# Batch 0's rows of three experts moved into the routing of batch 1, in a Perceiver layer with a mixture of experts

## Chip, cores and metric

The kernel runs on one core of a Trainium2 chip, in one launch. The metric is the device time of that core in microseconds (us). Before the change the median of three runs is 2997.42 us (2994.43 to 2998.41).

## What is computed

One layer in three steps, each added to x (2 batches of 512 tokens, 512 channels, float32): cross-attention to 8192 context tokens, causal self-attention, and a mixture of 16 experts with two experts for each token. The change lies in the third step:

```python
cap = int(LOAD * K * max(1, T / E))                      # 64 places for each expert and batch
g = jnp.einsum('btc,ce->bte', x, w_router)               # x: after a layer norm
gate_probs = jax.nn.softmax(g, axis=-1)
top_k_probs, positions, indices, expert_inputs = jax.vmap(lambda xb, pb: _dispatch(xb, pb, cap))(x, gate_probs)
expert_inputs = jnp.swapaxes(expert_inputs, 0, 1).reshape(E, B * cap, C)
gg = jnp.einsum('enc,ech->enh', expert_inputs, w_gate)
h = jnp.einsum('enc,ech->enh', expert_inputs, w_fc)
h = jax.nn.silu(gg) * h
o = jnp.einsum('enh,ehc->enc', h, w_proj)
expert_outputs = jnp.swapaxes(o.reshape(E, B, cap, C), 0, 1)
y = jax.vmap(_collect)(expert_outputs, indices, positions, top_k_probs)   # weighted sum of two rows per token
```

A token gets a place in its expert by counting along the batch, so the places of a batch are known only when all its tokens have been routed. Each expert has 64 places for batch 0 and 64 for batch 1, 128 rows together.

## The kernel before

**The stages.** Cross-attention fills the first 2500 us or so, self-attention the next 300 (`self_attention`, L1148). Batch 0's routing (`route(0, ...)`, L756) is cut into pieces that are hung into the gaps of batch 1's self-attention (`attend(1, fill)`, L1536). Then the routing of batch 1 runs by itself (`in_line`, L895), the rows of all experts are fetched (L1540), the experts run one after another (`experts`, L936), and at the end each token gathers its two result rows.

**What sets the order.** Each engine works through its own queue in program order, which is the order in which the Python code records the instructions. Engines wait for each other through semaphores that the tile framework puts in where one reads what another writes, or where a buffer is used again. DMAs are issued from three queues: SP (weights, stores of normed rows, final output), ScalarE (result rows of the experts), POOL (the indirect ones, which pick rows by number).

**Routing of batch 1** (`in_line`). For each of four tiles of 128 tokens: the last projection of self-attention (`output`), the statistics of the layer norm, and one call of `between(i)`, which loads an expert's weights. The first three tiles are normed on ScalarE, stored to the tensor `normed` in HBM (L770) and turned on TensorE (`turn`, L193, four 128x128 transposes into a bank, which is then copied to SBUF); the last tile follows. The router (L792) multiplies the turned tokens, 128 at a time as the stationary operand, with the 16 columns of the router's weights. Then come the two best experts of each token on VectorE (`top_first`, `top_second`), the counting of places on TensorE (`counted`, L840 to L845), on VectorE a one-hot of the places (`ranked`, L849), and on TensorE the token number of each place (`numbered`, L876), which is written to `mo.token`: 64 rows for batch 0, 64 for batch 1, one column for each expert. `probabilities` ends it, and a tiny sigmoid (L923) loads ScalarE's table for the experts.

**Fetch** (L927). For each expert one indirect DMA on POOL picks the 128 rows named in its column of `mo.token` from `normed` into a quarter of a buffer `gx` (four buffers with four experts each).

**Experts** (L936). For each expert the rows are turned (`turned_tile`), multiplied with the gate weights `wg` and the weights `wf` (`expand`, L953: the weights are the stationary operand, 128x128 each, the 128 rows the moving columns), a sigmoid on ScalarE and two products on VectorE make `hT`, and `contract` (L966) multiplies it with `wp`, copies the result to SBUF and writes 64 rows to `results[0]` and 64 to `results[1]` in HBM. The loop turns two experts ahead and contracts one behind. A matmul in float32 shows in the trace as two passes, each with its own weight load: 32 passes for an expansion, four for a contraction.

**Weights and buffers.** `load(e)` (L715) takes three buffers of the pool `mid` (22 buffers of 128x1024 float32), freed in the order in which their last readers stand. Experts 0 to 2 are loaded early (L1514), 3 to 5 by `between` in the routing, and six ahead in the loop (L986). The pool `big` has ten buffers (`gx`, `xn`, `mxnT` and the exponentials of the attention). In the self-attention and the routing PSUM is a ring of eight banks (`Ring`, L200); the experts have their own PSUM pool, which takes the banks over.

**End.** After the last expert's results have landed, POOL gathers for batch 0, then for batch 1, for each of four tiles twice 128 rows (L998); VectorE adds each, weighted, to `xs` (L1001), and SP writes out each tile (L1002).

The calls that put the stages in order are these (from L1536):

```python
attend(1, fill)
assert not pieces
in_line = route(1, bank, "j", bank, split=True)
in_line(lambda i: output(1, i), lambda i: load(3 + i) if i < 3 else None)
for e in range(E):
    fetch(e)
```

Of the kernel before, what the change touches and what calls it, by code (L numbers as in the profile page):

```python
# [11 lines left out]
F32 = mybir.dt.float32  # L12
# [3 lines left out]
AF = mybir.ActivationFunctionType  # L16
# [26 lines left out]
def perceiver_kernel(ctx: ExitStack, tc: tile.TileContext, a, out: bass.AP):  # L43
# [668 lines left out]
    NQ = 4  # L712
    loaded, pk, get, gx = {}, {}, {}, []

# [41 lines left out]
    def route(b, ps, pstag, ps1, split=False):  # L756
# [91 lines left out]

        def ranked():  # L849

# [9 lines left out]
            for k in range(2):  # L860
                nc.vector.tensor_tensor(
                    hit[:, k],
                    pos[:, k].unsqueeze(2).to_broadcast([P, TB, CAP]),
                    mo.place.unsqueeze(1).to_broadcast([P, TB, CAP]),
                    ALU.is_equal,
                )
            nc.vector.tensor_reduce(slot, both, AX.X, ALU.add)

# [25 lines left out]

        def in_line(output, between):  # L895

            last = TB - 1
            for i in range(TB):
# [12 lines left out]
            tiles.normed(last)  # L911
            stored(last)

            def halves(dst, src):
                nc.scalar.copy(dst[:, :2], src[:, :2])
                nc.vector.tensor_copy(dst[:, 2:], src[:, 2:])

            turn(ps, pstag, tiles[last], mxnT[:, :, last * P :], halves)
            router()
            for f in found:  # L920
                f()

            nc.scalar.activation(tile("warm", [P, 1]), eps, AF.Sigmoid)  # L923

        return in_line if split else pieces + [router, *found]

    def fetch(e):  # L927

        q, i = divmod(e, NQ)
        if i == 0:  # L930
            gx.append(b8("gx", (P, NQ, D)))
        nc.gpsimd.indirect_dma_start(
            out=gx[q][:, i, :], out_offset=None, in_=normed, in_offset=at_row(mo.token[:, e : e + 1])
        )

    def experts():  # L936
        with ExitStack() as st:
# [3 lines left out]
            def turned_tile(e):  # L941
                q, i = divmod(e, NQ)
                bT = sm.tile([P, ND, P], F32, tag="bT", name="bT", bufs=3)
                turn(ps, "t", gx[q][:, i, :], bT, nc.vector.tensor_copy)
                return bT

            def expand(e, bT):
                wg, wf, _ = loaded[e]
                ph = ps.tile([P, 2, NF, P], F32, tag="a", name="ph")
                for j, w in enumerate((wg, wf)):  # L950
                    for f in range(NF):
                        for c in range(ND):
                            nc.tensor.matmul(  # L953
                                ph[:, j, f, :],
                                w[:, c, f * P : (f + 1) * P],
                                bT[:, c, :],
                                start=(c == 0),
                                stop=(c == ND - 1),
                            )
                hT = sm.tile([P, NF, P], F32, tag="hT", name="hT")  # L960
                nc.scalar.activation(hT, ph[:, 0], AF.Sigmoid)
# [4 lines left out]
            def contract(e, hT):  # L966
                wpj = loaded.pop(e)[2]
                po = ps.tile([P, D], F32, tag="o", name="po2")
                for f in range(NF):
                    nc.tensor.matmul(po, hT[:, f, :], wpj[:, f, :], start=(f == 0), stop=(f == NF - 1))  # L970
                res = sm.tile([P, D], F32, tag="res", name="res")
                nc.scalar.copy(res, po)
                for b in range(B):
                    nc.scalar.dma_start(
                        results[b][e * CAP : (e + 1) * CAP, :], res[b * CAP : (b + 1) * CAP, :]
                    )

            turned = {0: turned_tile(0), 1: turned_tile(1)}
            before_h = None
            for e in range(E):  # L980
# [3 lines left out]
                if before_h is not None:  # L984
                    contract(e - 1, before_h)
                    if e - 1 + NBUF < E:  # L986
                        load(e - 1 + NBUF)
                before_h = hT
            contract(E - 1, before_h)


            for b in range(B):
                for i in range(TB):
                    y = xs[:, b * TB + i, :]
                    pair = m4("r", (P, 2, D))
                    for k in range(2):
                        r = pair[:, k, :]
                        nc.gpsimd.indirect_dma_start(  # L998
                            out=r, out_offset=None, in_=results[b], in_offset=at_row(get[b][:, k, i : i + 1])
                        )  # L1000
                        nc.vector.scalar_tensor_tensor(y, r, pk[b][:, k, i : i + 1], y, ALU.mult, ALU.add)  # L1001
# [146 lines left out]
    def self_attention(finish_cross, mo_w):  # L1148
        with ExitStack() as st:
# [363 lines left out]
            first_maxima(1, *(lambda i=i: output(0, i) for i in range(4)))  # L1513
            for e in range(3):  # L1514
                load(e)
# [22 lines left out]
            in_line = route(1, bank, "j", bank, split=True)  # L1538
            in_line(lambda i: output(1, i), lambda i: load(3 + i) if i < 3 else None)
            for e in range(E):  # L1540
                fetch(e)

    finish_cross = cross_attention(xattn_tail)
# [38 lines left out]
```

## Time and profile before

| What | us |
|---|---|
| median of three runs (lowest, highest) | 2997.42 (2994.43, 2998.41) |
| the profiled execution's own time | 2998.28 |
| its span (first to last instruction) | 2996.6 |
| TensorE busy in it | 2912.9 |
| VectorE, ScalarE, POOL busy | 1960.1, 1397.1, 2177.5 |
| mean granted TensorE clock | 0.987 |
| first fetch of rows starts (L932) | 2855.29 |
| first row turned for an expert (L193) | 2859.16 |
| last result write issued (L974) | 2965.3 |
| first and last final gather start (L998) | 2967.91, 2988.38 |

A row of the time line names the start, the length, the engine, the line of the kernel, the operation, what is written and read, and how often; in brackets stands how long the engine was idle before it and what ended that. PE is TensorE's matmul, PEld its weight load, DVE VectorE, ACT ScalarE, SP the DMA queue on SyncE. A queue's name ends in q. In a row by stretch each engine's busy time is followed by its number of instructions; then come the granted TensorE clock (1.00 is full, 0.50 half), the DMA engines' busy share and what they moved in GB/s. The ends of matmuls are modelled, so the spacing of starts says more than a row's length.

### The profile page before, as it was taken

What the parts mean: (1) busy time and instruction counts of PE and PEld (TensorE: products, weight loads), DVE (VectorE), ACT (ScalarE), POOL (GpSimd) and SP (SyncE); (2) the same over time, 40 slices, a digit from 0 to 9 for tenths busy, and PEclk for the clock granted to TensorE, in tenths of its full rate; (3) what the DMA queues carried; (4) which work ended last, traced back from release to release, by engine and by line L of the source; (5) the groups of instructions that cost most, each with busy time, mean ns of one, the idle gap of its engine ahead of it and who ended that gap; (6) DMA issues with size and microseconds to landing.
All of it is one profiled execution on the core that took longest, in us unless ns stands there. A gap on an engine that the chain in (4) does not pass through costs nothing.

```text
span 2996.6 us, 65645 instructions
## 1 busy us (share of the span) xinstructions
PE 2912.9 (97%) x28459; PEld 1128.1 (38%) x28459; DVE 1960.1 (65%) x3292; ACT 1397.1 (47%) x2614; POOL 2177.5 (73%) x880
## 2 busy tenths in 40 slices
PE   7999999999999999999999999999999999999985
PEld 2333333333333333333333333333333332345574
DVE  5567776677777677766777777777767666556422
ACT  1345555555555555544555555555555436563311
POOL 1598888888888888978888888888888872012022
PEclk9999999999999999999999999999999999999988
DMA  3000000000000000000000000000000002001374
GB/s 124 1 24 2 24 2 24 1 24 2 24 3 23 5 21 9 17 1 24 2 24 1 24 1 24 1 24 1 24 2 1 29 29 72 1 29 62 103 249 138
DMA packets 48145, 89.73 MB, mean 30 GB/s; under 512 B 4720, under 2 KB 23152, under 8 KB 47856
## 3 DMA queue, kind: packets, MB, share of 16 engines
q1 hardware_dynamic: 40832, 70.31, 7.0%
q0 software_dynamic: 2752, 8.39, 0.9%
q10 hardware_dynamic: 4272, 6.83, 0.7%
q8 instruction: 223, 3.65, 0.5%
q14 instruction: 66, 0.54, 0.1%
HBM read 77.13 MB, written 8.39 MB: 29 GB/s over the span
## 4 chain that ended last, share of the span: by engine, by line
PE 93%; DVE 3%; ACT 1%; DMA 1%; issue 1%; POOL 0%; ACTq 0%; POOLq 0%; DVEq 0%
PE s L220 31%; PE s L449 18%; PE s L514 16%; PE s L462 15%; PE s L481 4%; PE s L1244 2%; PE ph L953 2%; PE s L541 2%; PE po L970 1%; DVE cm L471 1%; PE s L1338 1%; PE s L1379 1%; DVE acc L549 1%; DMA r<-results,get 0%; DVE acc L529 0%
## 5 line engine op out<-in xcount | busy, mean ns | idle before, releaser
L680 POOL TENSOR_TENSOR es<-es,e 128x2048 f32<-128x2048 f32 x374 | 1700.7, 4547 | 54.9 <-ACT e L483 38.1
L483 ACT ACTIVATE e<-s 128x512 f32<-128x512 f32 x2048 | 1057.4, 603 | 1111.0 <-PE s L481 1111.0
L471 DVE TENSOR_REDUCE cm<-s 128x1 f32<-128x512 f32 x2048 | 1271.0, 683 | 332.3 <-PE s L449 332.2
L449 PE MATMUL s<-k,qT 32*128 32x512 f32 x4096 | 588.1, 641 | 3.4 <-DVE cm L471 1.9
L462 PE MATMUL s<-qT,k 32*128 32x512 f32 x4096 | 554.8, 593 | 3.1 <-ACT e L483 2.3
L514 PE MATMUL s<-e,v 128*32 128x512 f32 x4096 | 495.3, 600 | 1.1 <-DVE cm L471 1.0
L680 POOL TENSOR_TENSOR es<-e 128x2048 f32<-128x2048 f32 x63 | 286.1, 4541 | 242.9 <-ACT e L483 242.9
L220 PE MATMUL s<-wkv,ctx 128*32 128x512 f32 x3072 | 365.4, 596 | 0.4
L220 PE MATMUL s<-ctx,wkv 128*32 128x512 f32 x3072 | 356.5, 597 | 0.5
L462 PEld LDWEIGHTS s<-qT,k 32*128 32x128 f32 x4096 | 282.3, 184 | 185.1 <-issue 106.3
L529 DVE TENSOR_TENSOR acc<-acc,s 128x512 f32<-128x512 f32 (+1 forms) x359 | 207.8, 604 | 138.6 <-PE s L514 138.1
L449 PEld LDWEIGHTS s<-k,qT 32*128 32x128 f32 x4096 | 161.8, 183 | 330.7 <-issue 259.0
L514 PEld LDWEIGHTS s<-e,v 128*32 128x32 f32 x4096 | 107.4, 109 | 320.0 <-DVE cm L471 160.9
L481 PE MATMUL s<-rows,mb 4*128 4x512 bf16 x2048 | 218.0, 376 | 0.0
L425 DVE SCALAR_TENSOR_TENSOR k<-s,kf,m 128x512 f32<-128x512 f32 x128 | 96.1, 751 | 171.7 <-PE s L220 171.7
L220 PEld LDWEIGHTS s<-ctx,wkv 128*32 128x32 f32 x3072 | 87.2, 109 | 236.5 <-issue 155.5
L220 PEld LDWEIGHTS s<-wkv,ctx 128*32 128x32 f32 x3072 | 86.9, 109 | 214.3 <-issue 125.9
L440 ACT COPY v<-s 128x512 f32<-128x512 f32 x128 | 74.9, 585 | 98.7 <-PE s L220 77.8
L537 DVE TENSOR_TENSOR acc<-acc,s 128x1024 f32<-128x1024 f32 x56 | 68.4, 1221 | 71.1 <-ACT s L536 71.1
L1325 POOL TENSOR_SCALAR_AFFINE_SELECT e<-e 128x512 f32<-128x512 f32 x32 | 22.3, 708 | 120.0 <-ACT e L1323 120.0
L481 PEld LDWEIGHTS <-mb 4*128 4x128 bf16 x2048 | 68.5, 93 | 105.5 <-issue 97.4
L1293 POOL TENSOR_TENSOR rest<-scm,parts 128x16 f32<-128x16 f32 x8 | 2.0, 253 | 124.3 <-DVE parts L1291 121.2
(277 smaller groups left out, 1917.0 us busy)
## 6 DMA issues: line engine op xcount, KB each, us to landing
ctx<-in_ctxT_dram SPq DMA_DIRECT2D x45, 512.0 KB
wg<-in_L_ffn_w_gate_dram SPq DMA_DIRECT2D x16, 512.0 KB
wf<-in_L_ffn_w_fc_dram SPq DMA_DIRECT2D x16, 512.0 KB
wp<-in_L_ffn_w_proj_dram SPq DMA_DIRECT2D x16, 512.0 KB
results<-res ACTq DMA_DIRECT2D x32, 128.0 KB
m<-in_mask_BxS_bf_dram SPq DMA_DIRECT2D x16, 128.0 KB
w_wq_phiT<-in_wq_phiT_dram SPq DMA_DIRECT2D x2, 1024.0 KB
w_wq_ampT<-in_wq_ampT_dram SPq DMA_DIRECT2D x2, 1024.0 KB
```

Source lines behind the costliest of these rows:

```text
L220: nc.tensor.matmul(out[q], lhsT[:, q], rhs, start=start, stop=stop)
L425: nc.vector.scalar_tensor_tensor(k[:, keys], bank, kf[:, g, b : b + 1], mask_tiles[i][:, keys], ALU.subtract, ALU.mult)
L440: nc.scalar.copy(v[:, kt % (NKT // 2), :], bank)
L449: nc.tensor.matmul(s, qT(chunks[i][0], g, r, slice(qt * P, (qt + 1) * P)), k_tiles[n][r, hf * S : (hf + 1) * S], start=True, stop=True,)
L462: nc.tensor.matmul(s, k_tiles[n][r, keys], qT(chunks[i][0], g, r, slice(0, S)), start=True, stop=False)
L471: nc.vector.tensor_reduce(cms[g][chunks[i][1] % 2][:, qt, j : j + 1, hf], ss[j], AX.X, ALU.max)
L481: nc.tensor.matmul(ss[j], bias_tiles[i][r4, keys], rows[r4, :], start=False, stop=True)
L483: nc.scalar.activation(e[:, j, :], ss[j], AF.Exp)
L514: nc.tensor.matmul(av[j * HD : (j + 1) * HD, :], v_tiles[i][kt // (NKT // 2)][:, kt % (NKT // 2), h * HD : (h + 1) * HD], e[:, j, :], star ...
L529: nc.vector.tensor_tensor(dst, dst, src, ALU.add)
L537: nc.vector.tensor_tensor(acc[g], acc[g], pa.unsqueeze(1).to_broadcast([P, 2, S]), ALU.mult)
L680: nc.gpsimd.tensor_tensor(es, first if kt == 1 else es, e, ALU.add)
```

## The change

Three of the sixteen experts (13, 14 and 15, `SPLIT`) are treated apart.

- Their weights are loaded first (where experts 0 to 2 were); 0 to 2 are loaded in the routing of batch 1 (where 3 to 5 were); 3 to 5 after the fetches. The weights of 13 to 15 are loaded a second time in the experts' loop.
- Ahead of batch 1's routing, POOL fetches batch 0's 64 rows of these experts.
- Within `in_line`, between the steps of the routing, each of the three *halves* is turned, expanded with 64 columns, and put through sigmoid and products. Its place in the order of TensorE's queue is written out.
- After the fetches of all experts, which stay at 128 rows each, the halves are contracted: two of them side by side in one bank, then the third. Their results go to `results[0]`.
- In the loop experts 13 to 15 turn, expand and contract batch 1's 64 rows alone and write to `results[1]` alone.
- The gathers of batch 0 are issued in the loop behind the contraction of expert 12; those of batch 1 behind the last expert. The additions and writes follow in the old order.

The core of the diff:

```diff
-        def in_line(output, between):
+        def in_line(output, between, halves):
+            first, second, third = halves
...
             tiles.normed(last)
             stored(last)
+            first.turned()
+            first.expanded(0)
+            first.expanded(1)
...
-            turn(ps, pstag, tiles[last], mxnT[:, :, last * P :], halves)
+            turn(ps, pstag, tiles[last], mxnT[:, :, last * P :], by_two)
+            second.turned()
             router()
-            for f in found:
-                f()
-
-            nc.scalar.activation(tile("warm", [P, 1]), eps, AF.Sigmoid)
+            top_first()
+            second.expanded(0)
+            second.expanded(1)
+            counted(0)
+            top_second()
+            counted(1)
+            for half in (first, second):
+                half.gate()
+            third.turned()
+            third.expanded(0)
+            ranked(lambda: [half.gated() for half in (first, second)])
+            numbered()
+            third.expanded(1)
+            third.gate()
+            third.gated()
+            probabilities()
...
+    class Half:
+        def turned(self):
+            q, i = divmod(self.e, NQ)
+            pt = self.bank()[:, : ND * CAP].rearrange("p (c n) -> p c n", c=ND)
+            for c in range(ND):
+                nc.tensor.transpose(pt[:, c, :], gx[q][:CAP, i, c * P : (c + 1) * P], ident[:CAP, :CAP])
+            nc.scalar.copy(self.bT, pt)
+        def expanded(self, j):
+            if j == 0:
+                self.ph = self.bank()[:, : 2 * NF * CAP].rearrange("p (j f n) -> p j f n", j=2, f=NF)
+            expert_products(self.ph, self.e, self.bT, j)
+        def gate(self):
+            nc.scalar.activation(self.hT, self.ph[:, 0], AF.Sigmoid)
+        def gated(self):
+            for j in range(2):
+                nc.vector.tensor_tensor(self.hT, self.hT, self.ph[:, j], ALU.mult)
+
+    def contract_halves(some, bank, res):
+        po = bank()
+        for f in range(NF):
+            for n, half in enumerate(some):
+                nc.tensor.matmul(
+                    po[n * CAP : (n + 1) * CAP, :],
+                    half.hT[:, f, :],
+                    loaded[half.e][2][:, f, :],
+                    start=(f == 0),
+                    stop=(f == NF - 1),
+                )
+        used = slice(0, len(some) * CAP)
+        nc.scalar.copy(res[used, :], po[used, :])
+        for n, half in enumerate(some):
+            del loaded[half.e]
+            nc.scalar.dma_start(
+                results[0][half.e * CAP : (half.e + 1) * CAP, :], res[n * CAP : (n + 1) * CAP, :]
+            )
...
+            def collect(b):
+                for i in range(TB):
+                    pairs[b, i] = m4("r", (P, 2, D))
+                    for k in range(2):
+                        nc.gpsimd.indirect_dma_start(
+                            out=pairs[b, i][:, k, :],
+                            out_offset=None,
+                            in_=results[b],
+                            in_offset=at_row(get[b][:, k, i : i + 1]),
+                        )
...
                     if e - 1 + NBUF < E:
                         load(e - 1 + NBUF)
+                    if e == SPLIT[0]:
+                        collect(0)
                 before_h = hT
             contract(E - 1, before_h)
+            collect(1)
...
-            for e in range(3):
+            for e in SPLIT:
                 load(e)
...
-            in_line(lambda i: output(1, i), lambda i: load(3 + i) if i < 3 else None)
+            for e in SPLIT:
+                fetch(e, 0)
+            room, res = b8("room"), b8("res")
+            halves = [
+                Half(e, bank, (room[:, n, : ND * CAP], room[:, n, ND * CAP : (ND + NF) * CAP]))
+                for n, e in enumerate(SPLIT)
+            ]
+            in_line(lambda i: output(1, i), lambda i: load(i) if i < 3 else None, halves)
             for e in range(E):
                 fetch(e)
+            for n, some in enumerate((halves[:2], halves[2:])):
+                contract_halves(some, bank, res[:, n, :])
+            for e in range(3, NBUF):
+                load(e)
```

`expert_products` is the loop over the two 128-column blocks and four 128-row blocks of a weight that `expand` had in it.

## The prediction

> **What bounds the kernel now.** I read the page first (busy time, the 40 slices, the chain), then the chain of waits, the time line and the busy time by stretch for the last 180 us, where all of the change lies. The first 2818 us stay as they are, instruction for instruction, in the order of the built programs.
>
> ```profile
> PE 2912.9 (97%) x28459; PEld 1128.1 (38%) x28459; DVE 1960.1 (65%) x3292; ACT 1397.1 (47%) x2614; POOL 2177.5 (73%) x880
> ```
>
> TensorE bounds the whole, and only the last slices have gaps. By stretch (us, busy time of PE, PEld, DVE, ACT, POOL, granted clock, DMA share, GB/s) the end is four stages: the routing of batch 1, the wait for the first fetched rows, the experts, the final gathers.
>
> ```profile
> 2833.35:2854.52 21.17, 15.89 (x89) 14.91 (x88) 8.14 (x30) 7.07 (x12) 0.00 (x0) 0.63 0.38 125
> 2854.52:2859.16 4.64, 0.00 (x0) 0.03 (x1) 0.94 (x8) 0.00 (x0) 2.96 (x3) 0.50 0.65 200
> 2859.16:2965.90 106.74, 98.11 (x640) 79.96 (x640) 23.36 (x48) 15.49 (x32) 12.28 (x13) 0.94 0.64 201
> 2965.90:2996.60 30.70, 0.00 (x0) 0.00 (x0) 11.95 (x16) 0.00 (x0) 16.85 (x16) 0.54 0.68 213
> ```
>
> The routing on TensorE (start, length, what, idle before it) has three holes, and the clock is at half from 2838.8 on:
>
> ```profile
> 2837.70 0.66 PE L193 MATMUL s<-ident,xn 128*128 128x128 f32 x4 [1.57 <-DVE xn L118]
> 2838.19 6.30 PE L792 MATMUL s<-wr,mxnT 128*128 128x16 f32 x32
> 2845.92 0.66 PE L840 MATMUL s<-oh,before 128*128 128x64 f32 x2 [1.44 <-DVE oh L804]
> 2852.45 1.86 PE L876 MATMUL s<-whose,hit 128*64 128x16 f32 x16 [1.26 <-DVE hit L861]
> 2859.16 2.21 PE L193 MATMUL pt<-ident,gx 128*128 128x128 f32 x8 [4.86 <-DMA gx<-normed,token]
> ```
>
> Two rows of the same kernel price what is put in. The first is batch 0's router at full clock, the others the same stretch by clock window: TensorE was busy throughout, with 16-column matmuls, and then the clock fell.
>
> ```profile
> 2796.91 3.65 PEld L792 LDWEIGHTS s<-wr,mxnT 128*128 128x128 f32 x32
> 2797.80:2801.20 3.40, 3.40 (x42) 3.20 (x45) 0.00 (x0) 0.00 (x0) 0.00 (x0) 1.00 0.00 0
> 2801.20:2804.70 3.50, 3.50 (x40) 1.69 (x32) 1.75 (x4) 0.00 (x0) 0.00 (x0) 0.51 0.02 5
> ```
>
> The final gathers go at POOL's pace, the last write ending at 2996.6:
>
> ```profile
> 2967.91 0.94 POOL L998 DMA_INDIRECT r<-results,get  x1 [92.81 <-DMA results<-res]
> 2977.60 0.95 POOL L998 DMA_INDIRECT r<-results,get  x1 [0.30 <-DMA r<-results,get]
> 2988.38 0.94 POOL L998 DMA_INDIRECT r<-results,get  x1 [0.30 <-issue]
> 2992.57 0.75 DVE L1001 SCALAR_TENSOR_TENSOR xs<-r,pk,xs 128x512 f32<-128x512 f32 x1 [0.16 <-DMA r<-results,get]
> ```
>
> **The tail (a gain).** Today 16 gathers start between 2967.91 and 2988.38, 1.36 us apart. Eight remain. The eighth of today starts 9.69 us after the first; its addition is done about 5 us later (2982.8), and a write ends 3.3 us after its addition (2993.32 to 2996.6). So the end comes 9.7 + 5.2 + 3.3 = 18.2 us after the first gather instead of 28.7: 10.5 us. The last expert writes one block instead of two, and one issue of 0.55 us (1.10 for two) leaves the path. The out-writes of batch 0, which disturb the late gathers today, are mostly gone by then: up to 2 more. I take **-12** (between -10.5 and -13). Batch 0's eight gathers sit before these on POOL: results of expert 12 land near 2955, eight at 1.27 end at 2965.2, just before batch 1's can start (2967.4). Their eight additions (8 x 0.75 = 6 us) wait in DVE's order behind expert 15's products (2961.9) and end near 2968.3, before batch 1's first (2970.7).
>
> **Experts 13 to 15 with half the columns (nothing).** Here a rule and a row part. The Trainium skill (TensorE: Matmul & The Clock Gate, "Wait — 56ns, not 53.3ns?") has warm matmuls spaced by their moving columns, so 64 columns would cost half of 128; 3 x 32 passes of 0.11 would save 5.3 us. But the router's 16-column passes take 3.65 / 32 = 0.114 us, no less than the 128-column passes of an expert (3.57 us for 32 in the chain, 0.112): every pass brings its own 128x128 weight load. I take 0. By the rule the same halves in the routing would also cost half.
>
> **The work put into the routing (a cost).** Ahead of the token numbers TensorE now has three turns (4 passes each) and 80 passes of 64 columns (32, 32 and 16). At full clock: 80 x 0.114 + 3 x 0.44 = 10.4 us. At half (0.22 from the chain's 1.79 us for 8 passes of L845, 0.85 for a turn): 17.6 + 2.6 = 20.2. The holes take little of it: of the first (1.57) some 0.6, since the expansion waits for ScalarE to copy the turned rows, behind copies that end at 2837.03; 1.44 and 1.26 of the others; less 0.7 for the third half's own turn and copy. So 2.6 us are hidden. Queued behind it on TensorE are the router (behind the first half), the counting (behind the second) and the numbering (behind 16 passes of the third), so the rest delays the token, all 16 fetches on POOL and the experts.
>
> What it costs hangs on the clock. At full clock throughout, today's own passes would shrink too: router 6.15 to 3.65, counting by 2.7, numbering 1.86 to 1.10, 6.0 in all. Three cases for the token:
> - clock lost at 2838.8, as today: 20.2 - 1.3 (12 passes before it) - 2.6 = +16.3
> - lost behind the router: 36 passes at full 4.1, the rest at half 12.3, router -2.5, holes -2.6: +11.3
> - never lost: 10.4 - 2.6 - 6.0 = +1.8
>
> The skill's rule (same page, "HAM oscillation — how this bites in real kernels") is that idle gaps beyond some 3.4 us cool TensorE; the holes here are shorter, and fewer with the change, so by it the clock would stay: +1.8. The rows 2797.80 to 2804.70 say otherwise: no idle at all, router passes, half clock for one window afterwards. The router stays as it was, 3.65 us at full clock, about a window long. I take the middle of the first two cases, **+13.8**, with +1.8 as the lower end. At half clock 64-column passes are about half idle in the array, so I don't expect them to win the clock back; 512-column contractions did (2879.7 to 2883.1).
>
> **Between token and first expert.** Today 4.64 us of nothing. Now: 16 passes (3.5), the pair's contraction (4 pairs of 512 columns side by side, 3.6 at half), the third's (1.8, warm again) and ScalarE's copy of its bank, for which the first expert's turn waits (0.9): 9.8, so 5.2 beyond the cover. If the cover were gone, all 9.8. The first expert then runs warm: 6.35 us today (2859.16 to 2865.51), 4.95 at full clock, -1.4. **+3.8**.
>
> **What is hidden.** DVE's six products (128x128, about 0.29 each by L858), four of them ahead of the token, run beside the third's 16 passes. ScalarE swaps tables as often as before. Three fetches of 64 rows go to POOL after 2818, where it idles 38.5 us. SP: experts 13 to 15 load first, and nine loads (experts 3 to 5) come behind the stores of normed, where load 6 and one more go today; their slots are freed by the halves' own passes. 4.7 MB at 320 GB/s are 15 us of a stretch with a DMA share of 0.38; expert 3 is needed at 2888. Cost 0, with some 20 us to spare. Three 64-row result writes on ScalarE's queue (0.55 each): 0.
>
> **Sum** against the profiled execution (span 2996.6, own time 2998.28): 13.8 + 3.8 - 12 = +5.6, so 3003.9; its time is 0.9 above the median of 2997.42, which becomes **3003**.
>
> **One unknown, a stall.** From 2868 to 2878 TensorE stands in the middle of an expert's second product, with nothing named as the cause, while fetches and a weight load share the DMA queues:
>
> ```profile
> 2869.87 0.49 PE L953 MATMUL ph<-bT,wf 128*128 128x128 f32 x3 [1.14 <-issue]
> 2871.99 0.50 PE L953 MATMUL ph<-bT,wf 128*128 128x128 f32 x3 [1.62 <-issue]
> 2874.82 0.37 PE L953 MATMUL ph<-bT,wf 128*128 128x128 f32 x1 [2.33 <-issue]
> ```
>
> It costs some 9 us, and 2 more at half clock. I let it stand (0). If it ends with the fetches, as it does today, it swallows the +3.8; if it doesn't come, -10.
>
> **Rivals.**
> - *Faster: the clock holds, or the stall swallows the work* (0.20). Held clock: +1.8, then 1.8 + 1.7 + 1.7 + 0.9 = 6.1 before the first expert, 1.5 beyond the cover less 1.4, so +0.1, and -12: -10, 2987; swallowed: about 2994 to 2999. For it: 64-column passes keep the array busier than holes. Against: the router rows.
> - *Slower: batch 0's gathers stall TensorE* (0.20). Indirect gathers now run beside experts 13 to 15 and their result writes, as the fetches did from 2868 on. Half as many, so +5, up to the full 10: 3008 to 3013. It decides from about 3 us of stall, as the rest is already near zero. Against: 2859 to 2867 had fetches and no stall.
> - *It doesn't do what it says*: batch 0's gathers are late, and batch 1's queue behind them on POOL. The margin is 2 us; five late would leave -7 of the tail, 3008. I count it with the slower rival.
>
> **How the numbers follow.** The likeliest case (0.60) is the half clock with the stall as today: 3003, own range 2999 to 3008 (the two clock cases and the tail's ends). What a measurement can tell from no change is 0.2%, 6 us: above 3003.4 is slower, below 2991.4 faster. The likeliest case is split at that line, 0.32 the same and 0.28 slower; the first rival gives 0.17 faster and 0.03 the same; the second 0.20 slower. Faster 0.17, same 0.35, slower 0.48. The range of 8 in 10 is 2988 to 3014.
>
> **What would show it.** Right: expansions of 64 columns spaced at 0.11 or 0.21 us; half clock from the router on; the first fetch on POOL at 2866 to 2873; the first expert's turn near 2877; the last 8 gathers within 11 us. Wrong: granted clock 1.00 through the counting; passes of half the length; a TensorE gap marked "issue" while batch 0's gathers run, or none in the first experts.

## The result, and the profile after

The changed kernel takes **3010.22 us** (median of six runs, 3007.49 to 3013.61); the kernel before, run beside it, 2997.14 (six runs, 2994.43 to 2998.41). The ratio is 1.0042, 95% interval 1.0032 to 1.0052: slower by 13.1 us, where +5.6 was forecast (3003, with 2988 to 3014 as the range of 8 in 10). The profiled execution has a span of 3009.8 against 2996.6, 13.2 more, so its stages can be added up. I cut both traces at the same five events: batch 0's token (VectorE writes the row numbers of its places, L879 before and L884 after), the end of the last woT matmul (the last projection of self-attention), batch 1's token, ScalarE's sigmoid of expert 12, that of expert 15, and the end.

| Stage, us | before | after | more | forecast |
|---|---|---|---|---|
| start to batch 0's token | 2817.99 | 2820.04 | +2.05 | 0 |
| to the end of woT | 15.36 | 19.65 | +4.29 | 0 |
| to batch 1's token | 20.99 | 31.67 | +10.68 | +13.8 |
| to expert 12's sigmoid | 89.52 | 92.00 | +2.48 | +3.8 |
| to expert 15's sigmoid | 16.75 | 18.89 | +2.14 | 0 |
| to the end | 35.99 | 27.55 | -8.44 | -12 |

The first row tells nothing of the change: the same changed kernel has batch 0's token at 2817.13 in a second profile (after_again, below), and over all the kernels below it lies anywhere from 2815.0 to 2824.2. The other five rows add up to 11.15.

The time line of the changed kernel around batch 0's three fetches (POOL, L959) shows the second row. What ended an engine's idle time stands in brackets; "remote" and "issue" mean that the trace shows no releaser.

```profile
2820.49 1.00 POOL L959 DMA_INDIRECT gx<-normed,token  x1 [1.65 <-DVE pos L885]
2821.25 2.76 PE L220 MATMUL s<-w_woT,soT 128*32 128x512 f32 x24
2823.01 0.91 POOL L959 DMA_INDIRECT gx<-normed,token  x1 [0.30 <-issue]
2824.09 0.72 DVE L1495 STREAM_TRANSPOSE srec<-s 128x512 f32<-128x512 f32 x1 [3.00 <-remote]
2826.62 13.06 PE L220 MATMUL s<-w_woT,soT 128*32 128x512 f32 x104 [2.61 <-DVE soT L1500]
```

In the kernel before, VectorE's transpose of the sums (srec) is released by TensorE and starts 0.41 us after VectorE's last piece of work:

```profile
2819.46 0.72 DVE L1399 STREAM_TRANSPOSE srec<-s 128x512 f32<-128x512 f32 x1 [0.41 <-PE s L1379]
```

In the changed kernel it starts at 2824.09, 0.2 us after POOL's third fetch has ended, though TensorE's sums end at 2821.43. TensorE runs out of chunks that don't need it, waits 2.61 us for soT, and then runs one clock window at half.

The stages of the changed kernel, with the columns of the prediction's second fence (granted clock, DMA share and GB/s at the end), answer to the four stages before:

```profile
2839.69:2871.50 31.81, 29.65 (x181) 28.26 (x182) 9.08 (x34) 8.49 (x16) 0.00 (x0) 0.68 0.46 156
2871.50:2881.03 9.53, 8.74 (x28) 4.68 (x29) 1.53 (x10) 1.44 (x3) 6.65 (x7) 0.64 0.89 275
2881.03:2991.44 110.41, 96.38 (x640) 77.83 (x640) 27.30 (x56) 15.15 (x32) 16.07 (x17) 0.95 0.71 232
2991.44:3009.80 18.36, 0.00 (x0) 0.00 (x0) 6.07 (x8) 0.00 (x0) 8.14 (x8) 0.50 0.54 171
```

The routing is 31.8 us and not 21.2, with a clock of 0.68. The wait for rows is full of work and twice as long. The final gathers and writes take 18.4 us and not 30.7. TensorE's rows within the routing:

```profile
2843.74 2.00 PE L971 MATMUL s<-room,wg 128*128 128x64 f32 x16 [0.84 <-ACT room L988]
2845.58 1.95 PE L971 MATMUL s<-room,wf 128*128 128x64 f32 x16
2848.29 4.51 PE L795 MATMUL s<-wr,mxnT 128*128 128x16 f32 x32
2856.09 3.62 PE L971 MATMUL s<-room,wf 128*128 128x64 f32 x16
2865.83 3.68 PE L971 MATMUL s<-room,wg 128*128 128x64 f32 x16 [0.46 <-ACT room L988]
2881.03 1.09 PE L1033 MATMUL pt<-ident,gx 128*128 128x128 f32 x8 [0.79 <-ACT res L1015]
```

The first half runs at full clock. The clock falls at 2851.1, behind most of the router, and stays at half until 2878.4: the same 16 passes take 3.6 us instead of 1.8. The last lines of the changed kernel's time line, ahead of batch 1's gathers:

```profile
2982.25 0.28 ACT L1044 ACTIVATE hT<-ph 128x128 f32<-128x128 f32 x1 [4.80 <-remote]
2983.27 1.90 PE L1054 MATMUL po<-wp,hT 128*64 128x512 f32 x4 [0.86 <-issue]
2984.41 0.58 ACT L1056 COPY res<-po 64x512 f32<-64x512 f32 x1 [1.89 <-remote]
2987.22 0.45 ACTq L1058 DMA_DIRECT2D results<-res  x1
2991.44 0.94 POOL L1069 DMA_INDIRECT r<-results,get  x1 [6.62 <-DMA out_dram<-xs]
3000.78 0.94 POOL L1069 DMA_INDIRECT r<-results,get  x1 [0.30 <-issue]
```

Expert 15's sigmoid comes 1.8 us after its matmuls, and the copy of expert 14's result (2984.41) 1.9 us later than it could, both without a named releaser, while batch 0's gathers run on POOL (2975.13 to 2984.83). The last result takes 4.2 us from its issue to the first gather, 2.6 before.

### The profile page after: what moved, and what is told of

It reads as the page before. It is cut to its first block, busy times and chain, and to the rows that moved or that the text cites. A ratio compares the mean times of both kernels' runs of the same rounds, so it can differ in the third digit from the quotient of the medians.

```text
span 3009.8 us, 65933 instructions
## 1 busy us (share of the span) xinstructions
PE 2937.4 (98%) x28579; PEld 1144.9 (38%) x28579; DVE 1959.0 (65%) x3298; ACT 1399.5 (46%) x2621; POOL 2178.9 (72%) x883
## 4 chain that ended last, share of the span: by engine, by line
PE 93%; DVE 3%; issue 1%; ACT 1%; DMA 1%; POOL 0%; another core or an unknown queue 0%; POOLq 0%; ACTq 0%; DVEq 0%
PE s L220 31%; PE s L449 17%; PE s L514 16%; PE s L462 15%; PE s L481 4%; PE s L1340 2%; PE ph L971 2%; PE s L541 2%; PE po L1054 1%; DVE cm L471 1%; PE s L1434 1%; DVE acc L549 1%; PE s L1475 1%; PE s L971 0%; DVE acc L529 0%
```

## The experiments

Four kernels ran beside the kernel before in each of three sets. In the first of them (plain_fetch, fetches_only, collect_late, early_alone) every kernel, the kernel before too (2987.15 us), was 10 us shorter than in the others (2997.25 and 2999.36). So ratios are taken within a set, and so are stages where the set has a trace to compare with; the other stages are set against the first trace of the kernel before. The record names another chip for each set. I started with the theory that indirect fetches on POOL hold the other engines up (A), against the rival that they cost nothing (B), and took the clock (C and D) and the tail (E and F) after that.

**plain_fetch: the changed kernel, its three fetches made by plain DMAs.** They take rows 0 to 191 as they lie; the picking of the rows is left out.

```diff
-                fetch(e, 0)
+                nc.sync.dma_start(gx[q][:CAP, i, :], normed[i * CAP : (i + 1) * CAP, :])
```

> The changed kernel, with batch 0's three fetches of 64 rows made by plain DMAs from SP's queue (rows 0 to 191 of normed in place of the picked ones; the picking for the three halves is left out). Theory A (the indirect fetches on POOL hold VectorE up: in the changed kernel VectorE's transpose of srec starts at 2824.09 with 3.00 us of idle, 0.17 us after POOL's third fetch ends, against 0.41 us of idle before): the idle time falls back to about 0.4, the woT matmuls end 2.6 to 4.3 us earlier, the time is about 3006 to 3007.5. Theory B (POOL's fetches have no part in it; the 4.3 us belong to the clock window or to the loads): the transpose still waits about 3 us, the time stays 3010 within 1.5.

**fetches_only: the kernel before, with three fetches added.**

```diff
             in_line = route(1, bank, "j", bank, split=True)
+            spare = b8("spare", (P, NQ, D))
+            for n in range(3):
+                nc.gpsimd.indirect_dma_start(
+                    out=spare[:CAP, n, :],
+                    out_offset=None,
+                    in_=normed[:S, :],
+                    in_offset=at_row(mo.token[:CAP, E - 3 + n : E - 2 + n]),
+                )
```

> The kernel before, with nothing added but three indirect fetches of batch 0's 64 rows for experts 13 to 15 into a spare buffer, at the place where the change has them. Theory A (fetches on POOL hold VectorE up by about 2.6 us, and the gap it leaves on TensorE costs a half-clock window of up to 1.7 more): 2.6 to 4.3 us longer, 2999.7 to 3001.4. Theory B (fetches cost nothing, as predicted): 2997 within 1.5.

Measured: plain_fetch 2998.01 us, ratio 1.0035 (1.0021 to 1.0049); fetches_only 2987.53, ratio 1.0003 (0.9995 to 1.0011). The fetches alone cost nothing here, plain ones win nothing that stands out against the 1.0040 of collect_late below, and theory A seems to fall. But the time line of fetches_only says what kind of set this was:

```profile
2815.43 1.00 POOL L1541 DMA_INDIRECT spare<-normed,token  x1 [1.64 <-DVE pos L880]
2816.44 0.72 DVE L1399 STREAM_TRANSPOSE srec<-s 128x512 f32<-128x512 f32 x1 [0.41 <-PE s L1379]
2864.80 0.39 ACT L961 ACTIVATE hT<-ph 128x256 f32<-128x256 f32 x1 [19.59 <-PE ph L953]
```

VectorE goes on at once beside the fetches, and the first sigmoid of the experts comes 7.94 us after the first turn (2856.86). In the first trace of the kernel before it took 14.41 (first turn at 2859.16):

```profile
2873.57 0.38 ACT L961 ACTIVATE hT<-ph 128x256 f32<-128x256 f32 x1 [25.42 <-issue]
```

So the late releases in the main fetches, which the prediction saw as a stall of 9 us, are missing in all four traces of this set. They account for most of its 10 us: from batch 1's token to expert 12's sigmoid fetches_only takes 80.35 us, the first trace of before 89.52.

**collect_late: meant to put batch 0's gathers behind expert 15.**

```diff
-                    if e == SPLIT[0]:
-                        collect(0)
...
             contract(E - 1, before_h)
+            collect(0)
             collect(1)
```

> The changed kernel, with batch 0's eight gathers moved from behind the contraction of expert 12 to behind that of expert 15. If the tail's terms read from the two traces hold (10.3 us won by eight gathers fewer at the end, 3.8 lost by the gathers and writes that run beside experts 14 and 15): 3010.2 + 10.3 - 3.8 = about 3016.7, ScalarE's sigmoid of expert 15 and the landing of the last result back at 0.3 to 0.5 us of idle and 2.6 us. If the gathers beside the experts cost nothing (as predicted): about 3020.5 to 3022. If most of the gain is not theirs: under 3014.

Measured: 2999.09, ratio 1.0040 (1.0026 to 1.0054). As an experiment on the tail it failed: nothing stands ahead of these gathers on POOL, and they wait only for `results[0]`, so they started at 2962.88 all the same, beside experts 14 and 15. So the miss tells nothing of the tail's terms. It shows instead what the change costs where the late releases are missing. By stage against fetches_only: woT 0, routing +15.84, to expert 12 +1.38, to expert 15 +0.48, end -6.85, in all 10.9. That is about the same ratio as in the result's own runs, from other terms.

**early_alone: the kernel before with the early gathers, without halves.** Batch 0's rows of experts 13 to 15 are left out; rows of expert 0 stand in for them.

```diff
-                for b in range(B):
+                if e == 0:
+                    for late in range(E - 3, E):
+                        nc.scalar.dma_start(results[0][late * CAP : (late + 1) * CAP, :], res[:CAP, :])
+                for b in (1,) if e >= E - 3 else range(B):
...
+                    if e == E - 3:
+                        collect(0)
```

> The kernel before, with nothing but the early gathers: batch 0's gathers issued behind the contraction of expert 12, and experts 13 to 15 write batch 1's rows alone (batch 0's rows of these three are left out, expert 0's stand in for them). It shows what the change could win if the halves cost nothing. By the terms of the two traces: 2997.1 - 10.3 + 3.8 = about 2990.6. By the prediction's own sum for the tail (-12): 2985. If the gathers stall TensorE as the main fetches do (5 to 10 us): 2990 to 2995 with a gap of several us in TensorE's rows of experts 14 and 15.

Measured: 2982.53, ratio 0.9984 (0.9977 to 0.9991), 4.6 us faster. The end, from expert 15's sigmoid on, is 27.76 us against 35.91 in fetches_only: -8.15. My stand-in writes probably spoil the sum: the next pair of issues on ScalarE's queue, at 2874.27, took 9.21 us, and from the first turn to expert 12's sigmoid the kernel took 4.7 us longer than fetches_only. If that loss is theirs, the change could win about 8 us with the halves for nothing. No gap shows in TensorE's rows of experts 14 and 15 in this set.

**after_again: the changed kernel unchanged**, in the second set.

> The changed kernel as it is, on another chip or at another time than its first profile. Theory A (the stall of some 9 us in the fetches and VectorE's 3.00 us of idle ahead of srec belong to the chip or the moment, since four kernels of the first set showed neither): no such stall, the kernel before 10 us faster as well, and the ratio still 1.004: about 12 us over the kernel before of the same set, of it +15 to +16 at the token, +4 to the first expert's turn, -7 to -8.5 from the last expert's sigmoid to the last gather. Theory B (the stall belongs to the kernel): the first set's stall shows again, ScalarE's first sigmoid of the experts over 10 us late.

Measured: 3013.18, ratio 1.0053 (1.0039 to 1.0067). The late releases are back: 2.93 us ahead of srec, and the sigmoid of expert 0 comes 14.71 us after the first turn. They belong to the set, not to the kernel; since every set ran on another chip and at another time, the runs can't tell which of the two it is. By stage against the first trace of before: woT +4.22, routing +16.11, to expert 12 +1.54, to expert 15 +2.04, end -8.65. The routing differs from the first profile because the clock fell 5.2 us behind woT's end, ahead of the router, and not 11.4 behind it. The first row covers the first 31.81 us of a routing of 37.10:

```profile
2836.71:2868.52 31.81, 29.66 (x149) 28.20 (x150) 7.65 (x28) 8.49 (x16) 0.00 (x0) 0.58 0.45 149
2848.24 7.01 PE L795 MATMUL s<-wr,mxnT 128*128 128x16 f32 x32
```

The router takes 7.01 us here and 4.51 in the first profile.

**wide: halves of 128 columns.** Each of the 64 rows stands twice, and half of every product is not used.

```diff
-            nc.scalar.copy(self.bT, pt)
+            nc.scalar.copy(
+                self.bT.rearrange("p c (k n) -> p c k n", k=2), pt.unsqueeze(2).to_broadcast([P, ND, 2, CAP])
+            )
...
-                self.ph = self.bank()[:, : 2 * NF * CAP].rearrange("p (j f n) -> p j f n", j=2, f=NF)
+                self.ph = self.bank().rearrange("p (j f n) -> p j f n", j=2, f=NF)
...
-            nc.scalar.activation(self.hT, self.ph[:, 0], AF.Sigmoid)
+            nc.scalar.activation(self.hT, self.ph[:, 0, :, :CAP], AF.Sigmoid)
```

> The changed kernel with halves of 128 columns: each of the 64 rows stands twice in the turned tile, and only the first 64 columns of a product are used. No pass is added, each one moves twice the columns. Theory C (TensorE's clock follows how many columns move, and a pass costs its weight load whatever the columns): the passes of the halves win the clock back from half to full within a window or two, stay at about 0.11 us apart, and the token comes 6 to 10 us earlier than in the unchanged kernel of this set: about 6 to 10 us faster. Theory D (columns cost time, or the clock is lost for other reasons, such as the gaps): the passes take as long as before or longer and the time stays within 2 us or rises.

Measured: 3001.04, ratio 1.0015 (1.0008 to 1.0021), 12 us less than after_again in the same set. Twice the columns, and faster. TensorE's rows of the third half and the numbering in wide:

```profile
2862.04 2.05 PE L971 MATMUL s<-room,wg 128*128 128x128 f32 x16 [0.67 <-ACT room L988]
2864.03 1.10 PE L881 MATMUL s<-whose,hit 128*64 128x16 f32 x16
```

Two stretches of wide, with granted clock, DMA share and GB/s at the end:

```profile
2853.70:2857.10 3.40, 3.40 (x19) 3.40 (x18) 2.24 (x11) 3.09 (x4) 0.00 (x0) 0.51 0.03 9
2857.10:2874.00 16.90, 13.57 (x103) 10.28 (x102) 5.07 (x22) 2.30 (x5) 6.09 (x7) 1.00 0.69 217
```

The clock falls twice, from 2843.5 to 2846.9 and behind the router for another window of 3.4 us (0.51 in the first of the two stretches), and each time the passes of a half win it back. The third half's 16 passes take 1.99 us from start to start (2862.04 to 2864.03), against 3.60 in the changed kernel (2865.83 to 2869.43). The routing is +5.3, where after_again has +16.1 and the first profile +10.7. Theory C holds, D is out.

**writes_late: batch 0's output written behind batch 1's.**

```diff
-                    nc.sync.dma_start(out[b, i * P : (i + 1) * P, :], y)
+                    if b == 1:
+                        nc.sync.dma_start(out[b, i * P : (i + 1) * P, :], y)
+            for i in range(TB):
+                nc.sync.dma_start(out[0, i * P : (i + 1) * P, :], xs[:, i, :])
```

> The changed kernel, with the four writes of batch 0's output issued behind those of batch 1. Theory E (batch 0's out-writes lie before the last result write on the DMA queues; the last result takes 5.3 us from issue to batch 1's first gather in the other traces of the change, 3.1 without them): back to about 3.1, 2 us won there, but four writes of 256 KB more behind the last one, 1 to 3 us lost at the end: within 2 us. Theory F (the gathers themselves delay the landing): still about 5 us, and 1 to 3 us slower.

Measured: 3012.69, ratio 1.0057 (1.0044 to 1.0071). The end of its time line:

```profile
2980.69 0.45 ACTq L1058 DMA_DIRECT2D results<-res  x1
2983.90 0.94 POOL L1069 DMA_INDIRECT r<-results,get  x1 [4.94 <-DMA results<-res]
```

The last result takes 3.2 us to the first gather, against 4.6 in after_again, and the end comes 10.95 us after the last gather, against 8.17. Theory E as expected: the writes can be moved, but they cost their time at one place or the other. This trace has the other case of the clock, too: it fell 10.6 us behind woT's end, in the router, and the routing is +11.36, in the same set as after_again's +16.11.

**two_halves: experts 14 and 15 apart.**

```diff
-    SPLIT = range(E - 3, E)
+    SPLIT = range(E - 2, E)
...
-            third.turned()
-            third.expanded(0)
...
-            third.expanded(1)
-            third.gate()
-            third.gated()
```

> The changed kernel with two experts treated apart (14 and 15) instead of three; batch 0's gathers then start behind expert 13. If the terms add: the third half's 16 passes ahead of the token at half clock (3.4 us, with its turn 4.2) and its 16 passes, contraction and copy ahead of the first expert (3.4 + 1.8 + 0.6 = 5.8, of which some is cover: 3.7 over cover are lost in the changed kernel) fall away, 7 to 8 us; the gathers of batch 0 start 5.7 us later and end about when the last result lands, 0 to 2 lost: 5 to 8 us faster than the unchanged one of this set. If the cost is a fixed one (the clock's loss, the order), less than 3.

Measured: 3002.84, ratio 1.0023 (1.0017 to 1.0030), 10 us less than after_again. In its trace the routing is +11.20, the first turn comes 4.89 us behind the token (8.98 in after_again), and the way to expert 15 is -0.3. The end, 29.99, is 2.65 longer than with three: batch 0's gathers last until 2983.06 and batch 1's begin at 2984.31, though the last result was issued at 2977.79. The routing is 4.9 shorter than after_again's, where the clock also fell ahead of the router; 4.2 was expected for the third half. The whole is more than the 5 to 8 expected: between experts 12 and 15 only 0.24 are lost (2.04 in after_again), now that batch 0's gathers begin behind expert 15's sigmoid, at 2973.89. The third half was not worth its price.

**fetch_held: batch 0's fetches held until soT is written.**

```diff
-                fetch(e, 0)
+                nc.gpsimd.tensor_copy(gx[q][:1, i, :1], oT[1][:1, ND - 1, :1])
+                fetch(e, 0)
```

> The changed kernel, with batch 0's three fetches held back: a copy of one number on POOL ahead of each fetch waits for the last product of the attention (soT), so that the fetches run beside the woT matmuls and not beside the transposes ahead of them. Theory A (on the chips that show it, VectorE is released late while POOL's fetches run: 2.2 to 3.0 us of idle ahead of srec, woT's end 1.8 to 4.3 us later): the idle is back at 0.41 and the time 1.8 to 4.3 us shorter than the changed kernel's ratio of 1.0042 to 1.0053, so about 1.004. Theory G (whatever VectorE or ScalarE does beside the fetches is released late): the idle shows up at the next VectorE work, the additions to xs, and little or nothing is won. On a chip that shows no such idle in the other kernels: no difference.

Measured: 3012.23, ratio 1.0043 (1.0029 to 1.0057). In the trace srec's idle is 0.41 again and woT ends 15.36 us after the token: 4.3 less than in the first profile, 1.9 less than in wide_both of the same set. But the clock fell 5.6 us behind woT's end, and the routing is +15.70. The time is no shorter than the interval can tell: inconclusive on the time. Theory A names the right place; what the time won there is worth in the whole isn't shown.

**router_wide: the kernel before, its router with 128 columns.**

```diff
-                        banks["pl"][:, i, :E],
+                        banks["pl"][:, i, :],
...
-                        mo.wr[:, c, :],
+                        mo.wr[:, c, :].unsqueeze(1).to_broadcast([P, P // E, E]),
```

> The kernel before, with nothing changed but the router's moving operand: its 16 columns stand 8 times side by side (a repeated read, 128 columns), and only the first 16 are used. As many passes and weight loads as before. Theory C (the clock follows the columns that move; a pass costs its weight load): the half clock that begins at 2838.8 in the router comes later, in the counting; the router's 32 passes take 3.65 us and not 6.3; 2.5 to 4 us faster. Theory D (columns cost time, or the gaps make the clock fall): no gain, or slower.

Measured: 2995.26, ratio 0.9989 (0.9982 to 0.9995): faster than the kernel before by 4.1 us.

```profile
2841.48 5.21 PE L792 MATMUL s<-wr,mxnT 128*128 128x128 f32 x32
2849.01 1.08 PE L845 MATMUL s<-oh,ones 128*128 128x64 f32 x8
```

The detail was missed: the clock still falls near 2841, with the hole of 1.57 us ahead of the router, but the router's own columns win it back at 2844.6. The router takes 5.21 us and not 6.3, the counting behind it runs at full clock (1.08 for L845's eight passes, 1.9 at half in the trace of before), and the routing is -2.83. It does not last: the clock falls again at 2851.4.

**wide_both: both widenings in the changed kernel**, those of wide and this one:

```diff
-                        mo.wr[:, c, :],
+                        mo.wr[:, c, :].unsqueeze(1).to_broadcast([P, P // E, E]),
```

> The changed kernel with halves of 128 columns (as in wide) and the router of 128 columns (as in router_wide): the clock is held as far as columns can hold it, and the three halves are as in the change. The prediction's rival 'the clock holds' gave -10 against the kernel before. By the terms measured since: the token +5 to +7 and not +15 to +20, first turn +1.5, tail -7 to -8.5 from the last sigmoid on, 2 to 4 for VectorE's late release beside the fetches where the chip shows it: +1 to +4 against the kernel before, about 2 us faster than wide's 1.0015.

Measured: 3002.37, ratio 1.0011 (1.0005 to 1.0018). The clock is 1.00 from the routing's start to 2872, and the routing is 23.06 us, +2.07 against the kernel before. The prediction's case "never lost" had +1.8. The end is -7.4; but the fetches' late releases hold the experts until 16.94 us after the first turn (14.41 in before), and they take another 2.15 between experts 12 and 15.

**two_wide_held: two halves, both widenings, held fetches**, the edits of two_halves, wide_both and fetch_held together:

```diff
-    SPLIT = range(E - 3, E)
+    SPLIT = range(E - 2, E)
...
-                fetch(e, 0)
+                nc.gpsimd.tensor_copy(gx[q][:1, i, :1], oT[1][:1, ND - 1, :1])
+                fetch(e, 0)
```

> The best that the runs point to: two experts treated apart (as in two_halves), halves and router of 128 columns, batch 0's fetches held back. If the terms add: token +2 to +4 against the kernel before, first turn +0, from expert 12's sigmoid to the last gather -6.5 (as in two_halves): 2 to 5 us faster than the kernel before, about 0.9985. If holding the fetches brings nothing: 0 to -2. If the clock is lost in the counting all the same: +2 to +4.

Measured: 2996.99, ratio 0.9993 (0.9985 to 1.0002). Routing +1.02, end -7.65, to expert 12 +1.32. No difference from the kernel before can be told. Of the kernels that compute the whole layer, only router_wide, without the change, is clearly faster than the kernel before; the two intervals overlap, so which of these two is faster isn't shown.

## Why the prediction was right or wrong

**The routing (+13.8 forecast): right, mechanism and size.** The three cases of the clock were +16.3, +11.3 and +1.8. The runs showed all three: +16.11 in after_again (and +15.54 to +15.84 in the first set, +15.70 in fetch_held), +10.68 in the first profile and +11.36 in writes_late, and +2.07 in wide_both, where the clock was held. Which of the first two comes depends on where the clock falls, and that changes from run to run (after_again and writes_late, in one set). The Trainium skill's rule (TensorE: Matmul & The Clock Gate, "HAM oscillation — how this bites in real kernels"), which looks at idle gaps of TensorE, does not reach this case: wide loses the clock behind a router that ran without a gap, and wins it back by passes that only move more columns.

**64 columns cost a full pass: right.** At full clock 16 passes of 64 columns took 1.84 us (2843.74 to 2845.58 in the first profile's time line), 0.115 each, and 128-column ones 0.112 in the experts. At half clock 0.225. What the prediction didn't see is the other side of it: columns that cost nothing could have been put there.

**Token to first expert (+3.8): the local size was right, its effect smaller.** The first turn came +4.85 later, and the first expert ran 1.2 shorter (5.18 us to the next turn, 6.35 before). But at expert 12 only +1.4 to +2.6 were left in every trace with three halves. In after, after_again, wide, two_halves and two_wide_held ScalarE's first sigmoid comes 3.8 to 4.3 us after the last of the 16 fetches starts, which is 23.4 to 24.0 us after the token, wherever the first turn lies (4.6 to 9.7 us after it). So part of a later first turn is hidden in that wait. In the kernel before that sigmoid comes 19.2 us after the token, but half clock then lasts 10.2 us in the first experts (2872.9 to 2883.1), in the changed kernel 6.8 (2892.0 to 2898.8). "It swallows the +3.8" was named as a possibility and came half true. Where the releases are not late, the warm first expert was worth more than the 1.4 forecast: from first turn to first sigmoid 5.4 us in collect_late, at full clock, against 7.9 in fetches_only, at a mean clock of 0.60.

**"What is hidden": the step that failed.** "Three fetches of 64 rows go to POOL after 2818, where it idles 38.5 us", at cost 0: POOL was indeed idle, but I asked only what the fetches wait for and not what VectorE does beside them. It cost +4.29 in the first profile and +1.8 to +4.2 in the other sets with late releases, 0 in the set without them and where the fetches were held (fetch_held). Why the engines are released late stays open.

**The experts 13 to 15 and the slower rival: half right.** +2.14 between experts 12 and 15, and the rival "batch 0's gathers stall TensorE" had said +5 to +10. It looks like the late release beside the fetches, but it hits one sigmoid and one copy, since the gathers are through before more is due. In the first set it is +0.48, and +0.24 in two_halves and two_wide_held, where the gathers begin behind expert 15's sigmoid.

**The tail (-12): mis-sized.** The end shrank by 8.44 (by 6.85 to 8.81 in the other traces with three halves). Its working: from the first to the last gather 20.47 became 9.34, -11.13; the landing of the last result 2.58 became 4.22, +1.64; from the last gather to the end 8.22 became 9.02, +0.80; from the sigmoid to the last issue 4.72 became 4.97, +0.25, although one issue of 0.55 was saved. I had taken batch 0's out-writes as a disturbance that goes away, up to -2; writes_late shows that they moved in front of the last result write. The condition "eight at 1.27 end just before batch 1's" was met.

**The sum.** Forecast 13.8 + 3.8 - 12 = +5.6. Measured in the profile: 10.68 + 2.48 + 2.14 - 8.44 + 4.29 = +11.15, with 2.05 of scatter 13.2. The missing 5.6 are the fetches' 4.3, the last experts' 2.1 and the tail's 3.6, less 3.1 for the routing's luckier clock and 1.3 on the way to expert 12. So it was right that the change costs more than it wins, and with the routing's clock for the reason that was given; that the total missed by no more than 7.5 us is in part luck, as 10 us of missed costs met 4.4 of forecast costs that didn't come. The rival "clock holds, -10" had the routing right at +1.8, but even with it the kernel stays slower (wide_both), for the tail and the late releases.

## What to carry to other kernels

Before filling a hole in TensorE's order with narrow matmuls, ask at which clock they will run and what they leave behind: a float32 pass took as long with 16 or 64 moving columns as with 128, so more columns came for nothing, and those columns kept the clock (routing +16 became +2, and the kernel before gained 4 us by a repeated read in its router). Work that is pulled ahead of the last stage brings its own gathers and writes with it; put them into the sum of what the last result still has to pass. An idle engine's DMA issue is not free until you have looked at what the other engines do in those microseconds.

## What the runs showed of the hardware

**Engines that are released late beside indirect DMAs.** In the result's own runs and in two of the three sets VectorE, ScalarE and TensorE stood without a named releaser while POOL issued indirect DMAs: 2.2 to 3.0 us ahead of srec beside three fetches, some 9 us beside the sixteen (14.4 us from first turn to first sigmoid in after, 5.4 in collect_late), 1.8 beside the gathers. ScalarE's first sigmoid of the experts in the first profile after:

```profile
2891.06 0.95 POOL L959 DMA_INDIRECT gx<-normed,token  x1 [0.30 <-issue]
2895.39 0.38 ACT L1044 ACTIVATE hT<-ph 128x256 f32<-128x256 f32 x1 [14.42 <-remote]
```

The same sigmoid in collect_late, where it is released by TensorE's matmuls:

```profile
2883.98 0.38 ACT L1044 ACTIVATE hT<-ph 128x256 f32<-128x256 f32 x1 [5.43 <-PE ph L971]
```

In the set of plain_fetch hardly any of it showed, and all was 10 us shorter. Plain DMAs in the fetches' place ran only in that set, so they don't tell whether it is the indirect kind that does it. In fetch_held the three fetches ran beside the woT matmuls and the additions to xs, and these ended no later than without fetches (15.36 us after the token, as in before). What holds the engines stays open.

**The clock.** It fell and rose at places that differ from run to run, and stayed at half for about 3.4 us (2853.7 to 2857.1 in wide) or multiples of it. It came back with 128-column passes, not with 64-column ones (at half from 2851.1 to 2878.4 in the first profile after, until the contractions of 512 columns), although TensorE was busy 29.65 of the routing's 31.81 us. What makes it fall is less clear: behind a router of 16 columns without a gap in wide, but near holes of 0.8 to 1.6 us ahead of the router in router_wide and after_again.
